# One attention kernel, its side work at steps of its own, maxima and denominators spread over the partitions by DRAM

## The chip, the cores and the metric

The kernel runs on one core of a Trainium2 chip. A core has a matrix engine (TensorE, PE in the profile, with its weight loads as PEld), a vector engine (VectorE, DVE), a scalar engine (ScalarE, ACT), a general engine (GpSimd, POOL) and SyncE (SP), which issues most DMAs. Each engine works through its instructions in the order in which they were written, and waits on semaphores for the others. Matrix products go to PSUM, 8 banks of 2 KB per partition; everything else lies in SBUF or in DRAM. The metric is the time of one execution on the device, in microseconds (us).

## The reference

Four cross-attention layers follow each other on x (2048 tokens of 256 values) with one context (1601 tokens of 512 values). Layers 0, 2 and 3 are alike and called masked here:

```python
q = hidden_states @ Wq            # 16 heads of 64
k = encoder_hidden_states @ Wk
v = encoder_hidden_states @ Wv
logits = jnp.einsum('bhqd,bhkd->bhqk', q, k) * scale
# the columns of a few tokens get -20 * (1 - mask) of the query
probs = jax.nn.softmax(logits + col_bias, axis=-1)
out = jnp.einsum('bhqk,bhkd->bhqd', probs, v)
x = out.reshape(...) @ Wo + bo + x
```

Layer 1, called grouped, normalises x first, has 16 query heads of 16 values over 4 key heads, no mask, and adds its result to x too. All is 32-bit floating point.

## The kernel before, in words

A *block* is two heads of a masked layer (8 blocks a layer) or four of the grouped one (4 blocks, worked two heads at a time). A *unit* is one block, or one pair of heads, for 512 queries: 96 masked and 32 grouped units. A unit has 13 *chunks* of 128 keys (the last has 65).

One loop walks over all chunks of all units; one turn is a *step*. A step does three things for three different units: scores of a chunk of the newest unit (L751), exp of a chunk of the unit before (L834 subtracts the query's maximum on DVE, L841 takes exp on ACT), and the product with the values for a chunk whose exp was done one step earlier (L869). `DELAY` is the number of steps between a unit's last scores and its first exp, here 2; the step of a unit is counted from 0 to 12 by its scores.

In a masked layer scores lie transposed, keys on the partitions: ACT copies them out of PSUM (L763) and DVE keeps the maximum over chunks, still separate for each partition (L768). At step 0 of the next unit PE transposes these (L805), DVE reduces them to one value a query (`ntop`, L806), and at step 1 PE spreads the values over all partitions by transposing broadcast columns (L818) into the PSUM tile `b`, which the subtractions read. POOL adds the probabilities of the chunks (L844 for the first two together, L846 for the others) into `sums`; PE transposes the sums (L888), DVE reduces and inverts them (L889, L890), POOL spreads them along the free axis (`by`, L899), PE transposes that (L907), and DVE multiplies the unit's result with it (L911). Two products with Wo follow (L917), added to x by DVE (L923). In the grouped layer the denominators come out of the product with the values (L894), and maxima are subtracted within the score product.

What is not the pipeline itself is a *piece*: the queries of the next unit (L420), the finish of a unit just named, and the projections of the next block's keys (L369, in slices of 512 columns) and values (L384, chunk by chunk, two to a tile). The class `Pieces` holds queues of them (`urgent`, `fill`, `later`) and hands out about one a step, after the step's three parts. Every product of a piece goes to one PSUM tile, `pm` (pool `ps_m`, one buffer of one bank); the scores, the transposes of the maxima and those of the sums share two tiles of two banks (`ps_s`). The probabilities have 17 buffers (`NP`). The context, transposed, lies in DRAM and comes by DMA in tiles `ct`, three buffers; weights have two buffers.

At the end the order as written is made binding for PE, ACT and DVE. POOL has few instructions and works in the order written too, and so does SP with its DMAs, up to some shifts.

## Time and profile before

| what | value |
| --- | --- |
| median of 3 runs | 5647.72 us (5645.32 to 5651.95) |
| profiled execution | 5653.54 us, its span 5651.8 us |
| PE busy | 5321.4 us, 94% |
| DVE busy | 4013.6 us, 71% |
| ACT busy | 3196.2 us, 57% |
| POOL busy | 2837.7 us, 50% |
| mean granted PE clock | 0.98 of full speed |
| DMA, share of 16 engines | about 15% |

In the profile's lines, L with a number is a line of the kernel. A group line gives the engine, the operation, the tiles written and read (out<-in), how often, the busy time in us and the mean of one in ns, then the idle time before it and what ended it. A line of waits says which engine waited at which line for whom: total us, times, longest. A timeline line gives the start, the time it took, the engine, the line and the tiles, and in brackets the idle time before it with what ended it. A line of DMA issues gives the number of issues, the size of one, and the median time from issue to landing.

### The profile page before, as it was taken

The page shows a single profiled execution, that of the slowest core. Times are in us where ns is not written, and L with a number is a line of the kernel's source. Part 1 is how long each engine was busy: PE and PEld are TensorE (multiplying, and loading weights), DVE is VectorE, ACT ScalarE, POOL GpSimd, SP SyncE. Part 2 cuts the span into 40 slices and gives each one's busy share as a digit, 9 for nine tenths or more (in the row PEclk, how much of TensorE's full clock was granted, in tenths as well). Part 3 has the DMA queues.
Part 4 walks back from the last instruction along what each step waited for, and adds up shares of the span by engine and source line. Part 5 has one row for each costly group of instructions (what it writes and reads, how often), then busy time and mean ns, then how long its engine had stood idle before and what let it go on. Part 6 is the DMA issues. An engine that isn't in the chain of part 4 may idle for free.

```text
span 5651.8 us, 59516 instructions
## 1 busy us (share of the span) xinstructions
PE 5321.4 (94%) x22444; PEld 1865.2 (33%) x22444; DVE 4013.6 (71%) x4140; ACT 3196.2 (57%) x3513; POOL 2837.7 (50%) x1380
## 2 busy tenths in 40 slices
PE   6999999998889999999999999999999999999997
PEld 3333333332323333233233333333333333333332
DVE  3777777777765555555567777777777777777786
ACT  2666666665433434333456666666666666666665
POOL 1766666665410000000056666666666666666676
PEclk8999999999889999999999999999999999999998
DMA  4112211111100000001012111212111121111100
GB/s 135 32 57 60 59 49 53 55 56 44 39 20 5 9 9 9 9 13 52 15 51 61 56 54 49 57 56 59 46 56 55 54 59 49 53 56 52 54 17 15
DMA packets 209744, 252.88 MB, mean 45 GB/s; under 512 B 43529, under 2 KB 155401, under 8 KB 209456
## 3 DMA queue, kind: packets, MB, share of 16 engines
q1 hardware_dynamic: 206192, 243.69, 14.8%
q8 instruction: 177, 2.90, 0.2%
q0 software_dynamic: 1152, 3.28, 0.2%
q10 hardware_dynamic: 2112, 2.10, 0.1%
q14 instruction: 111, 0.91, 0.1%
HBM read 235.27 MB, written 13.76 MB: 44 GB/s over the span
## 4 chain that ended last, share of the span: by engine, by line
PE 78%; ACT 7%; POOL 7%; DVE 5%; issue 2%; DMA 0%; SPq 0%; ACTq 0%; POOLq 0%; DVEq 0%
PE po L869 24%; PE s L751 20%; PE pm L384 6%; PE pm L369 5%; PE pm L917 5%; POOL sums L844 4%; ACT p L763 4%; ACT p L841 3%; POOL sums L846 3%; PE s L850 2%; PE s L784 2%; PE pm L420 2%; PE s L805 2%; PE b L818 2%; PE s L855 2%
## 5 line engine op out<-in xcount | busy, mean ns | idle before, releaser
L846 POOL TENSOR_TENSOR sums<-sums,p 128x1024 f32<-128x1024 f32 (+1 forms) x1056 | 2499.2, 2367 | 1097.9 <-ACT p L841 1084.8
L763 ACT COPY p<-s 128x1024 f32<-128x1024 f32 (+1 forms) x1248 | 1263.4, 1012 | 1434.0 <-PE s L751 1138.3
L869 PE MATMUL po<-p,v 128*64 128x512 f32 (+1 forms) x6656 | 1821.7, 626 | 36.5 <-ACT p L841 34.7
L768 DVE TENSOR_TENSOR top<-s,top 128x1024 f32<-128x1024 f32 (+1 forms) x1056 | 1291.5, 1223 | 753.9 <-ACT p L763 749.4
L751 PE MATMUL s<-q,kT 64*128 64x512 f32 (+1 forms) x4992 | 1426.3, 648 | 117.6 <-DVE top L768 116.4
L834 DVE TENSOR_TENSOR p<-p,b 128x1024 f32<-128x1024 f32 (+1 forms) x1248 | 1504.7, 1206 | 2.4 <-PE b L818 2.0
L841 ACT ACTIVATE p<-p 128x1024 f32<-128x1024 f32 (+1 forms) x1248 | 1321.5, 1059 | 110.3 <-DVE p L834 109.4
L869 PEld LDWEIGHTS po<-p,v 128*64 128x64 f32 (+1 forms) x6656 | 332.0, 136 | 1032.1 <-issue 698.9
L899 POOL COPY by<-rden 128x512 f32<-128x512 f32 x128 | 78.5, 613 | 1111.8 <-DVE rden L897 1083.9
L751 PEld LDWEIGHTS s<-q,kT 64*128 64x128 f32 (+1 forms) x4992 | 370.7, 182 | 732.7 <-issue 454.6
L859 ACT ACTIVATE p<-s 128x1024 f32<-128x1024 f32 (+1 forms) x283 | 289.8, 1024 | 451.0 <-PE s L855 450.9
L844 POOL TENSOR_TENSOR sums<-p 128x1024 f32<-128x1024 f32 x96 | 226.5, 2360 | 434.2 <-ACT p L841 434.2
L789 DVE TENSOR_REDUCE row_top<-s 128x2 f32<-128x1024 f32 x261 | 318.6, 1221 | 122.9 <-PE s L784 121.9
L384 PEld LDWEIGHTS pm<-wv,ct 128*128 128x128 f32 (+1 forms) x2392 | 284.7, 187 | 218.9 <-issue 215.9
L384 PE MATMUL pm<-wv,ct 128*128 128x128 f32 (+1 forms) x2392 | 337.6, 286 | 0.5 <-ACT v L389 0.5
L369 PE MATMUL pm<-ct,wk 128*128 128x512 f32 (+1 forms) x736 | 315.8, 544 | 2.7 <-ACT kT L374 2.7
L917 PE MATMUL pm<-o,wo 128*128 128x512 f32 x512 | 292.0, 653 | 7.1 <-DVE xs L923 2.9
L859 ACT ACTIVATE p<-b 128x1024 f32<-128x1024 f32 (+1 forms) x133 | 136.2, 1024 | 217.8 <-PE b L855 217.8
L923 DVE TENSOR_TENSOR xs<-pm,xs 128x512 f32<-128x512 f32 x232 | 158.4, 683 | 90.4 <-PE pm L917 90.4
L806 DVE TENSOR_REDUCE ntop<-s 128x8 f32<-128x1024 f32 x96 | 117.6, 1225 | 130.9 <-PE s L805 130.6
L789 DVE TENSOR_REDUCE row_top<-b 128x2 f32<-128x1024 f32 x123 | 150.2, 1221 | 62.2 <-PE b L784 61.6
L420 PE MATMUL pm<-xT,wq 128*128 128x512 f32 x336 | 188.5, 644 | 0.0
(191 smaller groups left out, 3279.2 us busy)
## 6 DMA issues: line engine op xcount, KB each, us to landing
ct<-ctxT SPq DMA_DIRECT2D x288, 512.0 KB, 3.8
xT<-xT SPq DMA_DIRECT2D x104, 512.0 KB, 3.5
ct<-ctxT SPq DMA_DIRECT2D x48, 130.0 KB, 2.6
wk<-in_L_xattn_Wk_dram SPq DMA_DIRECT2D x24, 256.0 KB, 4.4
wv<-in_L_xattn_Wv_dram SPq DMA_DIRECT2D x24, 256.0 KB, 3.1
xT<-xs SPq DMA_DIRECT2D x12, 512.0 KB, 2.6
wq<-in_L_xattn_Wq_dram SPq DMA_DIRECT2D x24, 128.0 KB, 2.1
wo<-in_L_xattn_Wo_dram SPq DMA_DIRECT2D x24, 128.0 KB, 2.1
```

The source lines that it names most:

```text
L369: nc.tensor.matmul(u.pk[:, :n], u.wk[:, k, :], ct(k, a, n), start=(k == 0), stop=(k == NCT - 1),)
L384: nc.tensor.matmul(u.pv[:m, c - c0, :], ct(k, a, m), u.wv[:, k, :], start=(k == 0), stop=(k == NCT - 1),)
L751: nc.tensor.matmul(s[:m, h, :], self.u.kT[r, a : a + m], self.q[r, :], start=True, stop=(a != TAIL),)
L763: nc.scalar.copy(p[:m], s[:m])
L768: nc.vector.tensor_tensor(self.top[:m], s[:m], self.top[:m], ALU.max)
L789: nc.vector.tensor_reduce(self.top[:, :, q, k : k + 1], s, AX.X, ALU.max)
L834: nc.vector.tensor_tensor(self.p[c][:m], self.p[c][:m], self.less[:m], ALU.add)
L841: nc.scalar.activation(p[:m], p[:m], AF.Exp)
L844: nc.gpsimd.tensor_tensor(self.sums, self.p[0], p, ALU.add)
L846: nc.gpsimd.tensor_tensor(self.sums[:m], self.sums[:m], p[:m], ALU.add)
L869: nc.tensor.matmul(self.po[r, :], u.v[:m, c, r], self.p[c][:m, h, :], start=(c == 0), stop=(c == NT - 1),)
L917: nc.tensor.matmul(py, wo[:, ts(k, P)], self.o, start=True, stop=True)
```

## The change

- `DELAY` becomes 4 and `NP` 19: exp runs four steps behind the last scores.
- Queries are taken in natural interleaved order: the four transposes of the maxima and of the sums take every fourth query (`columns`), so that partition p holds queries 4p to 4p+3.
- `on_all_partitions` writes such a [128, 2, 4] tile to DRAM (there it is in natural order) and reads it back broadcast over the partitions; SP issues both. The maxima go this way into `spread`, which ACT copies into PSUM at step 3 of the next unit; L818's transposes are gone. The reciprocals of the denominators go this way into `by`; POOL's copy, L907's transposes and DVE's multiply are gone, and POOL multiplies the unit's result in place.
- The transposes of the sums come in two halves, one head each, through `pm` in place of `ps_s`. POOL's sum begins with a copy of chunk 0.
- Keys are projected chunk by chunk (128 columns), values with one tile a chunk, queries in two halves of 256 columns. Each such piece fills and empties its own `pm` tile.
- `Pieces` now has pieces due at steps of their own (`at`), counted for the finish from the step of a unit's last values, which is step 4 of the unit two later: sums at 5 and 6, the multiply at 9, the products with Wo at 11 and 12; queries at 7 and 8; in the grouped layer, stacking at 10 and 11 and a last piece at 12. Chunks of keys and values fill in by a credit in units of cost. A step can hold a due piece and a chunk.
- `wk` and `wv` have one buffer; context tiles are always two chunks wide and loaded three tiles ahead. In the grouped layer the same classes of pieces are cut in the same way.

The core of the diff (blank lines left out):

```diff
-    NP = 17
+    NP = 19
...
-    def context_slice(a, n):
-        step = NCT if n <= 256 else NCT // 2
-        tiles = []
-        for k in range(0, NCT, step):
-            ct = work.tile([P, step, 2 * QB // step], FP, name="ct", bufs=3)
-            nc.sync.dma_start(out=ct[:, :, :n], in_=ctxT_dram[:, k : k + step, a : a + n])
-            tiles.append(ct)
-        return lambda k, b, m: tiles[k // step][:, k % step, b - a : b - a + m]
+    def context_slice(c, held):
+        a = TCH[c][0]
+        n = sum(m for _, m in TCH[c : c + 2])
+        ct = work.tile([P, NCT, 2 * P], FP, name="ct", bufs=3)
+        nc.sync.dma_start(out=ct[:, :, :n], in_=ctxT_dram[:, :, a : a + n])
+        for d in range(len(TCH[c : c + 2])):
+            held[c + d] = lambda k, d=d: ct[:, k, d * P : (d + 1) * P]
...
+            u.wk = weights.tile([P, NCT, P], FP, name="wk", bufs=1)
+            u.wv = weights.tile([P, NCT, P], FP, name="wv", bufs=1)
...
+        def projections(self, u):
+            def keys(c, ct):
                 if u.kT is None:
                     u.kT = heads.tile([P, T], FP, name="kT")
-                if k0 == 0:
-                    u.pk = ps_m.tile([P, 512], FP, name="pm")
-                ct = slices["k", i]
-                for k in range(k0, k1):
+                a, m = TCH[c]
+                pk = ps_m.tile([P, QB], FP, name="pm")[:, :m]
+                for k in range(NCT):
                     nc.tensor.matmul(
-                        u.pk[:, :n], u.wk[:, k, :], ct(k, a, n),
-                        start=(k == 0), stop=(k == NCT - 1),
+                        pk, u.wk[:, k, :], ct(k)[:, :m], start=(k == 0), stop=(k == NCT - 1)
                     )
-                if k1 == NCT:
-                    nc.scalar.copy(u.kT[:, a : a + n], u.pk[:, :n])
-            def values(c, c0, c1):
+                nc.scalar.copy(u.kT[:, a : a + m], pk)
+            def values(c, ct):
                 if u.v is None:
                     u.v = heads.tile([P, NT, P], FP, name="v")
-                if c == c0:
-                    u.pv = ps_m.tile([P, 2, P], FP, name="pm")
-                a, m = TCH[c]
-                ct = slices["v", c0]
+                m = TCH[c][1]
+                pv = ps_m.tile([P, QB], FP, name="pm")[:m, :P]
                 for k in range(NCT):
                     nc.tensor.matmul(
-                        u.pv[:m, c - c0, :], ct(k, a, m), u.wv[:, k, :],
-                        start=(k == 0), stop=(k == NCT - 1),
+                        pv, ct(k)[:, :m], u.wv[:, k, :], start=(k == 0), stop=(k == NCT - 1)
                     )
-                if c == c1 - 1:
-                    nc.scalar.copy(u.v[:m, c0:c1, :], u.pv[:m, : c1 - c0, :])
...
+                nc.scalar.copy(u.v[:m, c, :], pv)
...
+        def query_pieces(self, unit):
             xt = unit.transposed_x()
...
+            half = QB // 2
+            def queries(j):
+                if j == 0:
                     unit.q = heads.tile([P, QB], FP, name="q")
-                    nc.scalar.mul(unit.q, unit.pq, 64 ** -0.5)
-            return [[lambda k=k: queries(k) for k in range(NC)]]
+                part = ts(j, half)
+                pq = ps_m.tile([P, QB], FP, name="pm")[:, :half]
+                for k in range(NC):
+                    nc.tensor.matmul(
+                        pq, unit.u.wq[:, k, :], xt[:, k, part], start=(k == 0), stop=(k == NC - 1)
+                    )
+                nc.scalar.mul(unit.q[:, part], pq, 64 ** -0.5)
+            return [(7 + j, Piece(lambda j=j: queries(j), 1.0)) for j in range(2)]
...
+            return found + [
+                (10, Piece(lambda: stacked(0), 0.5)), (11, Piece(lambda: stacked(1), 0.5)),
+                (12, Piece(last, 0.25)),
+            ]
...
+        return [
+            (9, Piece(squares, 0.0)), (10, Piece(rms, 2.0)),
+            *((11 + q // 2, Piece(lambda q=q: divide(q), 0.0)) for q in range(QT)),
+        ]
...
+    def columns(q):
+        return slice(q, QB, QT)
+    def on_all_partitions(cols, to):
+        rows = dram.tile([2, P, QT], FP, name="cols", bufs=4)
+        with nc.allow_non_contiguous_dma(reason="1024 values, four at a time"):
+            nc.sync.dma_start(out=rows.rearrange("h p q -> p h q"), in_=cols)
+        for tile_, heads_ in to:
+            src = rows[heads_].rearrange("(o h) p q -> o (h p q)", o=1)
+            nc.sync.dma_start(out=tile_, in_=src.to_broadcast(tile_.shape))
...
-                        nc.tensor.transpose(pt[:, h, q, :], self.top[:, h, ts(q, P)], ident)
+                        nc.tensor.transpose(pt[:, h, q, :], self.top[:, h, columns(q)], ident)
                 nc.vector.tensor_reduce(ntop, pt, AX.X, ALU.max, negate=True)
+                self.spread = work.tile([P, 2, QB], FP, name="spread", bufs=1)
+                on_all_partitions(
+                    ntop, [(self.spread.rearrange("n h q -> n (h q)"), slice(0, 2))]
+                )
...
                 self.less = ps_b.tile([P, 2, QB], FP, name="b")
-                for h in range(2):
-                    for q in range(QT):
-                        nc.tensor.transpose(
-                            self.less[:, h, ts(q, P)],
-                            self.ntop[:, h, q : q + 1].to_broadcast((P, P)), ident,
-                        )
+                nc.scalar.copy(self.less, self.spread)
...
-                if c == 1:
+                if c == 0:
                     self.sums = work.tile([P, 2, QB], FP, name="sums")
-                    nc.gpsimd.tensor_tensor(self.sums, self.p[0], p, ALU.add)
-                elif c:
+                    nc.gpsimd.tensor_copy(self.sums, p)
+                else:
                     nc.gpsimd.tensor_tensor(self.sums[:m], self.sums[:m], p[:m], ALU.add)
...
-        def denominators(self):
-            rden = self.rden = small.tile([P, 2, QT], FP, name="rden")
+        def denominators(self, h):
+            if h == 0:
+                self.rden = small.tile([P, 2, QT], FP, name="rden")
+            rden = self.rden
             if self.masked:
-                pt = ps_s.tile([P, 2, QT, P], FP, name="s")
-                for h in range(2):
-                    for q in range(QT):
-                        nc.tensor.transpose(pt[:, h, q, :], self.sums[:, h, ts(q, P)], ident)
-                nc.vector.tensor_reduce(rden, pt, AX.X, ALU.add)
+                pt = ps_m.tile([P, QT, P], FP, name="pm")
+                for q in range(QT):
+                    nc.tensor.transpose(pt[:, q, :], self.sums[:, h, columns(q)], ident)
+                nc.vector.tensor_reduce(rden[:, h, :], pt, AX.X, ALU.add)
+                if h == 0:
+                    return
                 nc.vector.reciprocal(rden, rden)
             else:
                 pd = ps_m.tile([P, QT, 2], FP, name="pm")
                 for q in range(QT):
                     nc.tensor.matmul(
-                        pd[:, q, :], self.oT[:, ts(q, P)], den_rows, start=True, stop=True
+                        pd[:, q, :], self.oT[:, columns(q)], den_rows, start=True, stop=True
                     )
                 nc.vector.reciprocal(rden, pd.rearrange("p q h -> p h q"))
-            self.by = work.tile([P, QT, 2, 64], FP, name="by", bufs=1)
-            nc.gpsimd.tensor_copy(
-                self.by,
-                rden.rearrange("p h (q o) -> p q h o", o=1).to_broadcast((P, QT, 2, 64)),
+            self.by = work.tile([P, QB], FP, name="by", bufs=1)
+            on_all_partitions(
+                rden, [(self.by[self.rows(h)], slice(h, h + 1)) for h in range(2)]
             )
         def divide(self):
-            pr = ps_m.tile([P, QB], FP, name="pm")
-            for q in range(QT):
-                nc.tensor.transpose(
-                    pr[:, ts(q, P)], self.by[:, q].rearrange("p h o -> p (h o)"), ident
-                )
-            self.o = work.tile([P, QB], FP, name="o", bufs=1)
-            nc.vector.tensor_tensor(self.o, pr, self.oT, ALU.mult)
+            nc.gpsimd.tensor_tensor(self.oT, self.oT, self.by, ALU.mult)
...
+        def finish(self):
+            found = [(1 + h, Piece(lambda h=h: self.denominators(h), 0.5)) for h in range(2)]
+            if not self.masked:
+                found = [(1, Piece(lambda: self.denominators(0), 1.0))]
+            found.append((5, Piece(self.divide, 0.0)))
+            return found + [(7 + k, Piece(lambda k=k: self.project(k), 1.0)) for k in range(NC)]
...
+        def at(self, step, found):
+            for steps, piece in found:
+                self.due.setdefault(step + steps, []).append(piece)
+        def step(self, step, share, cost):
+            self.credit = max(min(self.credit + share - cost, 1.5), -1.5)
+            for piece in self.due.pop(step, ()):
+                piece.run()
+                self.credit -= piece.cost
+            while self.fill and self.credit >= self.fill[0].cost / 2:
+                piece = self.fill.popleft()
+                piece.run()
+                self.credit -= piece.cost
...
+        loads, held = deque(), {}
+        def chunks(make, cost):
+            def piece(c):
+                make(c, held[c])
+                if (c % 2 or c == NT - 1) and loads:
+                    loads.popleft()()
+            loads.extend(lambda c=c: context_slice(c, held) for c in range(0, NT, 2))
+            return [Piece(lambda c=c: piece(c), cost(TCH[c][1])) for c in range(NT)]
+        makers = layer.projections(nxt)
+        first, second = [], []
+        if makers:
+            first = chunks(makers[0], lambda m: m / P)
+            second = chunks(makers[1], lambda m: 1.0)
+            for _ in range(3):
+                loads.popleft()()
+        first += layer.own_keys(nxt)
...
-    DELAY, LAG = 2, 1
+    DELAY, LAG = 4, 1
...
+        if top and ca == DELAY - 1:
             top.maxima_spread()
-        if scoring and ca == 2 and ka + 1 < len(units):
+        if scoring and ca == 5 and ka + 1 < len(units):
             ahead = unit_of(ka + 1)
-            pieces.urgent.extend(ahead.layer.unit_groups(ahead))
+            pieces.at(step - ca, ahead.layer.query_pieces(ahead))
         if valuing and cv == NT - 1:
-            pieces.urgent.extend(valuing.finish_groups())
-            pieces.urgent.extend(after(kv))
-        if scoring and ca == 4 and units[ka - 1][:1] == units[ka][:1] != units[ka - 2][:1]:
-            pieces.fill.extend(pieces.later)
-            pieces.later.clear()
-        if scoring and not (top and top.masked):
-            i, b, sub = units[ka]
-            after_this = sum(u[0] == i for u in units[ka + 1 : ka + 8])
-            steps = NT - ca + (NT - 2) * after_this
-            pieces.step(max(1.0, (pieces.left() + 6 * after_this) / steps))
-        elif not scoring:
-            pieces.step(1.0)
-    pieces.flush(pieces.urgent)
+            pieces.at(step, valuing.finish() + after(kv))
+            if units[kv + 1 : kv + 2] and units[kv + 1][0] != units[kv][0]:
+                pieces.release()
+        share = 0.0
+        if scoring:
+            units_left = NB * len(scoring.layer.SUBS) - place - ca / NT
+            own = 6.0 if scoring.masked else 4.6
+            share = (pieces.left() + own * units_left) / (NT * units_left)
+        pieces.step(step, share, 1.0 if top and top.masked and ca == 0 else 0.0)
```

## The prediction

> **What bounds the kernel now.** I read the page's engine line and its chain first, then PE's waits, then the timeline of one unit of a masked layer, then the DMA list.
>
> ```profile
> PE 5321.4 (94%) x22444; PEld 1865.2 (33%) x22444; DVE 4013.6 (71%) x4140; ACT 3196.2 (57%) x3513; POOL 2837.7 (50%) x1380
> ...
> PE 78%; ACT 7%; POOL 7%; DVE 5%; issue 2%; DMA 0%; SPq 0%; ACTq 0%; POOLq 0%; DVEq 0%
> ```
>
> PE is busy 94%, yet it carries only 78% of the chain: other engines hold it up in places. PE's own waits name them.
>
> ```profile
> PE s L751 <- DVE top L768: 116.4, 71, 2.7
> PE pm L907 <- POOL by L899: 55.9, 79, 4.4
> PE po L869 <- ACT p L841: 34.7, 27, 4.1
> ```
>
> Those three make 207 of PE's 330 us of idle time (5651.8 - 5321.4). The list of all engines' waits shows what stands behind the first:
>
> ```profile
> ACT p L763 <- POOL sums L844: 174.5, 93, 2.5
> ```
>
> The buffer of probability chunk 0 is not free until POOL has added chunks 0 and 1. PE's timeline in a masked unit:
>
> ```profile
> 4026.48 1.09 PE L818 MATMUL b<-ident,ntop 128*128 128x128 f32 x8
> 4027.50 1.13 PE L751 MATMUL s<-q,kT 64*128 64x512 f32 x4
> ...
> 4035.82 1.09 PE L888 MATMUL s<-ident,sums 128*128 128x128 f32 x8
> 4038.62 1.13 PE L751 MATMUL s<-q,kT 64*128 64x512 f32 x4 [1.71 <-DVE top L768]
> 4039.68 1.08 PE L869 MATMUL po<-p,v 128*64 128x512 f32 x4
> 4041.38 0.66 PE L907 MATMUL pm<-ident,by 128*128 128x128 f32 x4 [0.62 <-POOL by L899]
> 4041.96 1.13 PE L751 MATMUL s<-q,kT 64*128 64x512 f32 x4
> ```
>
> From start to start, scores cost PE 1.06 us a step, values 1.01, the spread (L818) 1.02, the transposes of the reciprocals (L907) 0.58. The last view is one step on all engines, with a projection (L917) as its piece:
>
> ```profile
> 4002.32 1.13 PE L751 MATMUL s<-q,kT 64*128 64x512 f32 x4
> ...
> 4003.55 1.02 ACT L763 COPY p<-s 128x1024 f32<-128x1024 f32 x1 [1.15 <-PE s L751]
> 4004.39 1.13 PE L917 MATMUL pm<-o,wo 128*128 128x512 f32 x2
> ...
> 4004.60 1.22 DVE L768 TENSOR_TENSOR top<-s,top 128x1024 f32<-128x1024 f32 x1 [0.18 <-ACT p L763]
> ...
> 4005.74 0.68 DVE L923 TENSOR_TENSOR xs<-pm,xs 128x512 f32<-128x512 f32 x1
> ```
>
> Counted from the score's start, PE is done with its piece at 3.12, but DVE empties the piece's PSUM tile only at 4.10, because its maximum of the step stands ahead. There is one such tile ("pm"). A second piece in the same step must wait for it.
>
> **What it removes.** (a) The spread: 96 masked units x 1.01 = 97 us of PE. (b) The reciprocals' transposes: 96 x 0.58 + 32 x 0.49 (grouped layer, 2526.34 to 2526.83) = 71 us. (c) The wait on POOL's `by`: 56 us. (d) The wait behind L844: POOL now copies chunk 0 at once, the probability pool grows with the delay (17 to 19), and the sums' transposes leave the score buffers; of 116 I take 110. What is late next there is the values' wait for exp, below. Together 334 us. On DVE the multiply L911 goes too (88 us), which lies beside PE.
>
> **What it adds on PE.** The instruction order of both versions shows how many pieces fall into each step. Steps with two pieces, one after the other through the one "pm" tile:
>
> (e) 66 steps with half of the sums' transposes and then a chunk of K or V. A half takes 0.51 (half of L888), so the chunk could start at 1.06 + 1.01 + 0.51 = 2.58. DVE's half reduce, about 0.65 (half of 1.216, and the nearest 512-wide row is 0.68), follows the maximum, so the tile is free near 4.1: 1.55 x 66 = 102 us. Lower end 0.5 (POOL or DVE ahead of the row shown), upper 2.5.
>
> (f) 22 steps with a projection, then a V chunk: 4.15 - 3.12 = 1.0 each, 23 us.
>
> (g) Grouped layer, 63 steps with a projection, then a stacking piece: L917 at 2529.12, its DVE add 2530.28 to 2530.97, PE would go on at 2530.09: 0.95 x 63 = 60 us, and some 10 more doubles of its own key pieces, 10 us.
>
> (h) Chunk after chunk, emptied by ACT: 26 pairs, a burst of 13 V chunks before the second block, and the first block's 26 chunks. The rows for such waits are 0.3 us (L369 on kT, 2.7 us in 9) and 0.45 (L384 on v, 1.8 in 4): 0.4 x 65 = 26 us.
>
> (i) K in pieces of 128 columns: a V chunk costs 1.09 from start to start, a quarter of a K slice 1.055; 12 x 24 x 0.035 = 10 us. Queries in halves of 256 have no row; between 0 and 0.1 a unit, I take 5 us.
>
> (j) ACT's new copy into PSUM, 1.02 by L763, stands in its queue behind exp of chunk 12; DVE's first subtract and ACT's first exp wait for it, the copy of `oT` queues behind that, and the next unit's first values wait for both. In 25 units the next step has no piece, and there this comes to about 1 us: 25 us. DVE's two half reduces in neighbouring steps (3.1 and 3.3 us of DVE against 2.58 of PE) cost the 30 units without a double about 0.5: 15 us. Against them stand the 35 us of values' waits shown above, which belong to the old places: together +5 us.
>
> (k) Ends. Two steps more in the drain, where POOL binds at 2.45 a step, against two shorter at the start: 3 us. After the last sums the reciprocals go through DRAM in place of POOL and PE: some 4 us. In the last block, which has no chunks, POOL is near the bound; its copy (1.2, twice the 0.61 of L899) and multiply (1.2, half of 2.37) less `by` 0.61 make 1.8 x 4 = 7 us, and (a) and (b) gain nothing there: 6 us. Together 20 us.
>
> (l) At the change to the grouped layer two of the four normalising parts (0.94 + 2 x 0.64 each) share a step, where each had its own; DVE's sum is the same. I take 8 us, between 0 and 20.
>
> Sum of costs: 102 + 23 + 70 + 26 + 15 + 5 + 20 + 8 = 269. Net 334 - 269 = 65 us off the profiled execution's 5653.5 (span 5651.8 and 1.7 around it), that is 5588. That execution lies 6 us above the median of 5647.7, which is inside the runs' spread of 6.6; I say 5585.
>
> **The round trips at nothing.** Their cover is three steps. The new write (4 KB in pieces of 16 bytes) and the broadcast reads have no row; the nearest are
>
> ```profile
> ct<-ctxT SPq DMA_DIRECT2D x288, 512.0 KB, 3.8
> xT<-xT SPq DMA_DIRECT2D x104, 512.0 KB, 3.5
> ...
> wo<-in_L_xattn_wo_dram SPq DMA_DIRECT2D x16, 16.0 KB, 1.7
> ...
> ctxT<-p SPq DMA_DIRECT2D x2, 65.0 KB, 3.2
> tok_idx<-ttn_token_indices_A_dram SPq DMA_DIRECT2D x3, 1.0 KB, 3.2
> ```
>
> Write 1.7 to 3.2, read 512 KB 3.5 to 7.4 (the slowest 512 KB row of the list, the stores of ctxT). I take 2.4 + 3.6 = 6.0, near the rows of equal size in a quiet stretch (DMA is busy 15 to 20%). The maximum `ntop` is reduced 3.4 us into step 0; ACT's copy could start 3.2 us into step 3, and three steps are 7.2 to 9.4 us: cover 7.0 to 9.2 us. So it is hidden by 1 to 3 us, but at the upper end, 10.6, it is late by 1.4 to 3.6. On SP the write waits for DVE, the read for the write, and behind them the next ct load, which is not due for some steps. Ahead of them at a block's start stand wv and one or two ct loads (some 4 to 8 us of queue, issued one to two steps earlier). For the denominators the cover is longer: reciprocals at 4.4 us of step 6, POOL's multiply after its add at 5.7 of step 9, 14 us later less 4.4. POOL then multiplies until 7.0 of step 9, and PE projects at 7.3 or later; were `by` late, POOL's next adds would queue behind the multiply, and PE's projection behind both.
>
> wk and wv have one buffer each now. SP can load wk only after the last K chunk of the block before, which lies half a block back, and wv after the last V chunk; the first K chunk stands in step 1 to 3, the row for wk is 4.4 us, so this is hidden too. The ct loads stay as many, each of 512 KB.
>
> [...]
>
> **Rivals.**
> 1. *The trip through DRAM is late (slower).* ACT waits for it with the copies of the score buffers behind it, and PE with them. It decides from 65/96 = 0.7 us late in the mean unit on, a trip of about 8.8 us; at 10.6 it is 2.5 x 96 = 240 us, 5825; at 9.5, 1.4 x 96 = 134, about 5720. For it: two dependent transfers, a pattern not in the trace. Against: idle queues.
> 2. *The doubles cost half.* If DVE is ahead, or PE's wait overlaps a wait it has anyway, (e) to (g) are 98 instead of 195: 5490.
> 3. *The change is a wash.* The "pm" tile gives back all that PE saves: 3.0 us per double with a sum, (e) 198: 5681; at 2.5, 5650. For it: evacuations on DVE with a full queue.
> 4. *POOL becomes the bound*: its 12 adds of 2.37, copy and multiply are 31 us of a unit of 42. Only if the multiply beside DVE took 5 us and more; then some 5700. Little for it.
>
> **How the numbers follow.** Forecast (5540 to 5636) 0.46; rival 2 0.15; rival 1 0.22; rival 3 0.13; rival 4 0.04. What a measurement can tell from no change is 0.2%, 11 us. Faster: forecast and rival 2, 0.61, less a little of the forecast's upper end and with some of rival 3's lower: 0.60. Same 0.09, from rival 3 and the weak end of rival 1. Slower 0.31. The range goes from rival 2 (5490, and 10 for its spread) to rival 1 at 9.5 us with 20 for spread: 5480 to 5740. The forecast's own is 5540 to 5636.
>
> **What would show it.** In the new profile: no L818 and L907 groups; PE's wait for `top` near zero; new waits of "pm" matmuls on DVE `rden` and `xs` of about 1.5 and 1 us, some 66 and 85 times; ACT's copy of `spread` without a DMA wait; POOL copies of chunk 0. If ACT waits for the DMA of `spread`, rival 1 holds. If the waits on `rden` are far off 1.5 us, (e) is wrong.

## The result, and the profile after

The forecast was a gain of 1.1%. There is none: the kernel after took 5650.64 us (median of 12 executions, 5638.94 to 5661.18), the kernel before beside it 5649.26 us (12 executions, 5641.72 to 5655.72), a ratio of 1.0005 with an interval of 0.9996 to 1.0013. The profiled execution of after is the fastest of its twelve; its span is 5637.2 us, against 5651.8 before. The working below explains these 14.6 us between two spans; by the medians there is nothing to explain but a zero.

The engine line and the chain of the page after:

```profile
PE 5255.5 (93%) x23412; PEld 2070.8 (37%) x23412; DVE 3981.3 (71%) x4183; ACT 3346.0 (59%) x4096; POOL 3018.6 (54%) x1476
...
PE 80%; DVE 9%; ACT 7%; issue 3%; DMA 1%; POOL 0%; SPq 0%; ACTq 0%; POOLq 0%; DVEq 0%; another core or an unknown queue 0%
```

PE is busy for only 66 us less, although L818 and L907 are gone, and their transposes were 176 us. Its weight loads (PEld) take 206 us more, most because K in chunks of 128 columns and queries in halves load their weights more often (L369 2392 times for 736, 290.3 us for 111.8; L404 672 times for L420's 336, 113.8 us for 50.1), some for another reason that follows below. PE's own waits after, with total us, times and longest:

```profile
PE pm L380 <- DVE rden L893: 50.7, 40, 1.7
PE po L872 <- ACT p L844: 44.3, 39, 5.0
PE po L872 <- ACT oT L878: 33.4, 27, 4.2
PE pm L369 <- DVE rden L893: 32.4, 24, 1.5
PE pm L511 <- DVE xs L922: 22.7, 29, 0.8
PE pm L628 <- DVE xs L922: 22.7, 29, 0.8
PE pm L380 <- DVE xs L922: 20.6, 22, 1.0
```

The scores' wait for `top` and the wait for `by` are gone from the head of the list. In their place stand the doubles (two pieces in one step) that the prediction named: chunks of K and V behind half of the sums (`rden`), stackings (L511, L628) and V chunks behind a projection (`xs`). One such double in the timeline (start, duration, and in brackets the wait before):

```profile
4030.99 0.56 PEld L892 LDWEIGHTS pm<-ident,sums 128*128 128x128 f32 x4 [0.81 <-DVE rden L893]
4031.00 0.75 PE L892 MATMUL pm<-ident,sums 128*128 128x128 f32 x4
4031.33 1.22 DVE L772 TENSOR_TENSOR top<-s,top 128x1024 f32<-128x1024 f32 x1
...
4032.46 0.68 DVE L893 TENSOR_REDUCE rden<-pm 128x4 f32<-128x512 f32 x1
...
4033.20 1.16 PE L380 MATMUL pm<-wv,ct 128*128 128x128 f32 x8 [1.45 <-DVE rden L893]
```

DVE's maximum L772 stands in front of the half reduction L893, so `pm` comes free 1.45 us after PE could have used it, as the prediction argued. What it did not look at is in the groups. First the matrix products and weight loads before:

```profile
L888 PEld LDWEIGHTS s<-ident,sums 128*128 128x128 f32 x768 | 84.4, 141 | 84.9 <-issue 69.5 <-POOL sums L846 15.4
L894 PEld LDWEIGHTS pm<-den_rows,oT 128*128 128x128 f32 x256 | 31.0, 191 | 26.0 <-issue 25.2 <-ACT p L763 0.8
```

and the same work after, where the columns are every fourth query:

```profile
L892 PEld LDWEIGHTS pm<-ident,sums 128*128 128x128 f32 x768 | 108.2, 209 | 164.9 <-POOL sums L847 70.6 <-issue 47.7 <-DVE rden L893 36.9
L900 PEld LDWEIGHTS pm<-den_rows,oT 128*128 128x128 f32 x256 | 62.1, 327 | 26.8 <-issue 26.8
```

Each transpose has one weight load (768, eight in each of 96 units). With every fourth query, in steps of 16 bytes, one takes 209 ns instead of 141, and in the grouped denominators 327 instead of 191.

The table counts PE's time from the start of each product to the start of the next, less idle time, in the two profiled executions. With some 11 us ahead of the first and behind the last product it adds up to the spans.

| part of PE's time | before, us | after, us | difference |
| --- | --- | --- | --- |
| spread L818, transposes L907 | 176.4 | 0 | -176.4 |
| transposes of sums L888 / L892 | 103.0 | 137.3 | +34.3 |
| transposes of maxima L805 / L809 | 99.8 | 110.9 | +11.1 |
| grouped denominators L894 / L900 | 29.4 | 60.6 | +31.2 |
| K chunks L369 | 315.8 | 343.0 | +27.2 |
| V chunks L384 / L380 | 330.2 | 339.8 | +9.6 |
| projections L917 / L916 | 268.5 | 280.3 | +11.8 |
| scores and values | 3046.0 | 3026.8 | -19.2 |
| all other products | 951.9 | 956.4 | +4.5 |
| idle between products | 320.0 | 371.0 | +51.0 |

Scores and values are the same instructions in both kernels; the mean granted clock was 0.980 before and 0.984 after.

### The profile page after: what moved, and what is told of

Its sections match the earlier page's. It is cut to its first block, busy times and chain, and to the rows that moved or that the text cites. A ratio compares the mean times of both kernels' runs of the same rounds, so it can differ in the third digit from the quotient of the medians.

```text
span 5637.2 us, 63697 instructions
## 1 busy us (share of the span) xinstructions
PE 5255.5 (93%) x23412; PEld 2070.8 (37%) x23412; DVE 3981.3 (71%) x4183; ACT 3346.0 (59%) x4096; POOL 3018.6 (54%) x1476
## 3 DMA queue, kind: packets, MB, share of 16 engines
q1 hardware_dynamic: 338288, 328.53, 20.6%
q14 instruction: 127, 1.04, 0.1%
## 4 chain that ended last, share of the span: by engine, by line
PE 80%; DVE 9%; ACT 7%; issue 3%; DMA 1%; POOL 0%; SPq 0%; ACTq 0%; POOLq 0%; DVEq 0%; another core or an unknown queue 0%
PE po L872 24%; PE s L755 20%; PE pm L369 6%; PE pm L380 6%; PE pm L916 4%; PE pm L404 4%; ACT p L767 3%; DVE p L837 2%; PE s L853 2%; PE s L788 2%; PE s L809 2%; ACT p L844 2%; PE s L858 2%; DVE top L772 2%; PE pm L892 1%
## 5 line engine op out<-in xcount | busy, mean ns | idle before, releaser
L849 POOL TENSOR_TENSOR sums<-sums,p 128x1024 f32<-128x1024 f32 (+1 forms) x1152 | 2725.1, 2366 | 1089.6 <-ACT p L844 1012.1
L872 PE MATMUL po<-p,v 128*64 128x512 f32 (+1 forms) x6656 | 1813.3, 624 | 83.8 <-ACT p L844 44.3
L772 DVE TENSOR_TENSOR top<-s,top 128x1024 f32<-128x1024 f32 (+1 forms) x1056 | 1291.6, 1223 | 680.4 <-ACT p L767 678.6
L844 ACT ACTIVATE p<-p 128x1024 f32<-128x1024 f32 (+1 forms) x1248 | 1322.0, 1059 | 169.5 <-DVE p L837 163.3
L910 POOL TENSOR_TENSOR oT<-oT,by 128x512 f32<-128x512 f32 x128 | 163.8, 1280 | 1160.8 <-DMA by<-cols 901.1
L380 PE MATMUL pm<-wv,ct 128*128 128x128 f32 (+1 forms) x2392 | 344.4, 287 | 78.9 <-DVE rden L893 50.7
L380 PEld LDWEIGHTS pm<-wv,ct 128*128 128x128 f32 (+1 forms) x2392 | 286.6, 187 | 284.7 <-issue 142.0
L369 PE MATMUL pm<-ct,wk 128*128 128x128 f32 (+1 forms) x2392 | 346.0, 288 | 45.8 <-DVE rden L893 32.4
L369 PEld LDWEIGHTS pm<-ct,wk 128*128 128x128 f32 x2392 | 290.3, 191 | 258.3 <-issue 175.6
L916 PE MATMUL pm<-oT,wo 128*128 128x512 f32 x512 | 292.2, 653 | 13.3 <-POOL oT L910 12.5
L383 ACT COPY v<-pm 128x128 f32<-128x128 f32 (+1 forms) x312 | 82.2, 264 | 186.8 <-PE pm L380 179.0
L847 POOL COPY sums<-p 128x1024 f32<-128x1024 f32 x96 | 99.5, 1037 | 170.6 <-ACT p L844 170.6
```

The lines of the kernel that those rows point to most:

```text
L369: nc.tensor.matmul(pk, u.wk[:, k, :], ct(k)[:, :m], start=(k == 0), stop=(k == NCT - 1))
L380: nc.tensor.matmul(pv, ct(k)[:, :m], u.wv[:, k, :], start=(k == 0), stop=(k == NCT - 1))
L772: nc.vector.tensor_tensor(self.top[:m], s[:m], self.top[:m], ALU.max)
L844: nc.scalar.activation(p[:m], p[:m], AF.Exp)
L849: nc.gpsimd.tensor_tensor(self.sums[:m], self.sums[:m], p[:m], ALU.add)
L872: nc.tensor.matmul(self.po[r, :], u.v[:m, c, r], self.p[c][:m, h, :], start=(c == 0), stop=(c == NT - 1),)
```

## The experiments

Unless something else is said, each run was timed five times beside nine executions of the kernel before. Differences are taken between the ratios to before, one percent being 56.5 us.

**Consecutive queries in the denominators.** In the kernel after:

```diff
-                    nc.tensor.transpose(pt[:, q, :], self.sums[:, h, columns(q)], ident)
+                    nc.tensor.transpose(pt[:, q, :], self.sums[:, h, ts(q, P)], ident)
...
-                        pd[:, q, :], self.oT[:, columns(q)], den_rows, start=True, stop=True
+                        pd[:, q, :], self.oT[:, ts(q, P)], den_rows, start=True, stop=True
```

> Only the transposes of the sums (L892) and the denominators' products (L900) read consecutive queries again in place of every fourth, so that the denominators belong to the wrong queries; the maxima stay strided. Theory 1 (the stride makes PE's weight loads longer: in the changed kernel L892 takes 137 us of PE from start to start against 103 for L888 before, L900 61 against 29): 34 + 31 = 65 us less, about 5585, weight loads of L892 back from 209 to about 140 ns. Rival (PE waits for DVE in these steps anyway, so the masked part is hidden): 31 us less, about 5620. Rival (the stride is not the cause, the loads are long for another reason): no change, 5650.

Measured: 5613.11 us, ratio 0.9925 [0.9912, 0.9939], some 45 us below the kernel after. The same two groups of weight loads in this run:

```profile
L892 PEld LDWEIGHTS pm<-ident,sums 128*128 128x128 f32 x768 | 83.4, 145 | 167.5 <-POOL sums L847 69.0 <-issue 51.7 <-DVE rden L893 36.1
L900 PEld LDWEIGHTS pm<-den_rows,oT 128*128 128x128 f32 x256 | 31.8, 195 | 26.8 <-issue 26.8
```

The loads fall back to 145 and 195 ns: it is the stride. PE's time in L900 falls from 60.6 to 33.3, in L892 from 137.3 to 121.6 only. The other 19 us of L892 above the 103.0 of before stay. They probably go with the halves, in which four transposes instead of eight follow each other; no run has the halves alone, but the kernel before agrees: its transposes in fours (L907) took 0.154 us of PE each, its transposes in eights (L888) 0.134, and these, in fours, 0.158. And 8 us of the gain went back into the waits for `rden` (83 to 91 us): a chunk that is sooner at the tile waits longer for it.

**The same stride put into the kernel before.**

```diff
-                        nc.tensor.transpose(pt[:, h, q, :], self.sums[:, h, ts(q, P)], ident)
+                        nc.tensor.transpose(pt[:, h, q, :], self.sums[:, h, q::QT], ident)
...
-                        pd[:, q, :], self.oT[:, ts(q, P)], den_rows, start=True, stop=True
+                        pd[:, q, :], self.oT[:, q::QT], den_rows, start=True, stop=True
```

> The kernel before with one thing changed: the transposes of the sums (L888) and the grouped denominators' products (L894) load every fourth query instead of 128 in a row, as the change does. Nothing else moves. (What comes out belongs to other queries, so the denominators are put to wrong ones; the instructions are otherwise the same.) Theory (a strided load of a TensorE weight costs TensorE's time, whatever stands around it): L888 from 103 to about 119 us and L894 from 29 to about 60, 45 us in all above the kernel before. Rival (the difference seen between the two kernels came with the half tiles and the places of the pieces): within 10 us of the kernel before.

Measured: 5672.05 us beside 5644.91, ratio 1.0048 [1.0034, 1.0062], 27 us slower. In this run:

```profile
L888 PEld LDWEIGHTS s<-ident,sums 128*128 128x128 f32 x768 | 101.5, 208 | 83.9 <-issue 68.4 <-POOL sums L846 15.5
L894 PEld LDWEIGHTS pm<-den_rows,oT 128*128 128x128 f32 x256 | 62.2, 327 | 26.0 <-issue 25.1 <-ACT p L763 0.8
```

208 and 327 ns, with everything else as before: the stride alone makes the price, and the rival (half tiles and places) falls. PE's time is +12 us in L888 and +31 in L894. That is 43, of which 27 arrived; the scores' wait for `top`, which stands in other places of the same steps, was 10 us shorter, and scores and values ran 8 us faster. A load in steps of 16 bytes thus cost 67 and 136 ns more than one of consecutive values. No run tries another stride, and why this one costs it is not shown here.

**Consecutive queries everywhere, with the order made in DRAM.** In the kernel after all transposes read 128 consecutive queries, and the write to DRAM puts them in order:

```diff
-        return slice(q, QB, QT)
+        return ts(q, P)
...
-            nc.sync.dma_start(out=rows.rearrange("h p q -> p h q"), in_=cols)
+            nc.sync.dma_start(out=rows.rearrange("h q p -> p h q"), in_=cols)
```

> All three kinds of strided loads gone, and the order kept right by writing to DRAM in pieces of 4 bytes (1024 of them) in place of 16 bytes (256). Theory 1: 77 us less than the changed kernel, about 5573, if the longer write stays hidden; the write takes 2.4 us in the changed kernel, its cover is 1 to 3 us more. Rival (the write grows by more than 3 us): ACT's copy of spread waits for its DMA and the gain is eaten; from 0.8 us late in the mean unit on nothing is left.

Measured: 6922.08 us, ratio 1.2247 [1.2230, 1.2264]. The DMA issues (times, size, median us from issue to landing) and ACT's waits:

```profile
spread<-cols SPq DMA_DIRECT2D x96, 512.0 KB, 4.6
by<-cols SPq DMA_DIRECT2D x256, 128.0 KB, 3.9
...
cols<-rden SPq DMA_DIRECT2D x128, 4.0 KB, 10.1
cols<-ntop SPq DMA_DIRECT2D x96, 4.0 KB, 9.7
```

```profile
ACT p L767 <- POOL sums L849: 694.0, 195, 9.0
ACT b L824 <- DMA spread<-cols: 538.4, 93, 10.7
```

The same 4 KB in pieces of 4 bytes take 9.7 to 10.1 us to land; in the kernel after, in pieces of 16, 2.4. This is the prediction's first rival, made to happen: a trip of 9.7 + 4.6 = 14.3 us against a cover of 7.0 to 9.2, and with it a trip of 14.0 for the denominators, cost more than a fifth of the time before. Leaving out the waits over 20 us in and around the grouped layer, which both kernels have, POOL's multiply waited 765 us for `by` in 96 waits, against 50 in 16 in the kernel after, and ACT's copies of the scores waited for POOL's additions behind it. The clock was lower too, 0.899. The interleaved order is therefore no whim. It buys the write of 2.4 us and pays for it with the strided loads.

**No chunk in a step that has a due piece.** In `Pieces.step` of the kernel after:

```diff
-            for piece in self.due.pop(step, ()):
+            due = self.due.pop(step, ())
+            for piece in due:
...
-            while self.fill and self.credit >= self.fill[0].cost / 2:
+            busy = any(piece.cost for piece in due)
+            while not busy and self.fill and self.credit >= self.fill[0].cost / 2:
```

> The changed kernel, but a chunk of keys or values is not filled into a step that has a due piece with a cost: the 66 steps with a sum's transposes and a chunk are gone, 25 more pairs of chunks appear. Theory 1 (one PSUM tile, emptied by DVE behind its maximum): the 85 us of PE's waits on rden go, about 10 come back between chunks: 75 us less, about 5575. Rival (DVE is the bound in those two steps, 3.1 and 3.3 us against 2.7 of PE, and PE waits for exp instead): 35 us less, about 5615.

Measured: 5557.22 us, ratio 0.9833 [0.9819, 0.9846], 97 us below the kernel after. The waits for `rden` are gone from PE's list, whose next entries did not grow:

```profile
PE po L872 <- ACT p L844: 43.2, 40, 5.0
PE po L872 <- ACT oT L878: 23.2, 11, 4.2
PE pm L511 <- DVE xs L922: 22.7, 29, 0.8
PE pm L628 <- DVE xs L922: 22.7, 29, 0.8
PE pm L380 <- DVE xs L922: 20.5, 22, 0.9
```

So the chunks have room elsewhere, and the 66 doubles were a pure loss. The gain is 12 us more than their 85: the values' wait for `oT` fell by 10, for 17 chunks now stand in steps that had no piece (see (j) below). The 22 V chunks behind a projection stay (20.5 us): `flush` hands them out at the change of a block, which this edit leaves alone.

**Stackings moved away from the projections as well.** On top of the last edit:

```diff
-                (10, Piece(lambda: stacked(0), 0.5)), (11, Piece(lambda: stacked(1), 0.5)),
-                (12, Piece(last, 0.25)),
+                (9, Piece(lambda: stacked(0), 0.5)), (10, Piece(lambda: stacked(1), 0.5)),
+                (14, Piece(last, 0.25)),
```

> The kernel after, with no chunk of fill in a step that has a due piece with cost, and with the grouped queries' two stackings one step earlier and their last piece at step 14, so that they no longer stand directly behind a projection in `pm`. In the run with the first of these edits alone (5557 us) the stackings and the last piece still waited 52 us for the projections' additions (`pm` L511 and L628 <- DVE `xs` L920 and L922). Theory (these waits are a cost of where the pieces stand): they go, 5557 - 50 = about 5507 us. Rival (another piece stands behind the additions instead): within 15 us of 5557.

Measured: 5481.74 us beside 5648.31, ratio 0.9707 [0.9694, 0.9720], 71 us below the last run where 50 were expected. The waits of L511 and L628 for `xs` went, and PE's time in the projections came back to 269.5 us from 280: a stacking right behind a projection had cost there too. With these pieces apart the change is a gain of 2.9%.

**POOL's copy alone, in the kernel before.**

```diff
-                if c == 1:
+                if c == 0:
...
-                    nc.gpsimd.tensor_tensor(self.sums, self.p[0], p, ALU.add)
-                elif c:
+                    nc.gpsimd.tensor_copy(self.sums, p)
+                else:
```

> The kernel before with one edit: POOL copies chunk 0 into the sums in place of adding chunks 0 and 1 together. This is term (d) alone. Theory 1 (the stall at the sums is the buffer of chunk 0 held by POOL): PE's 116 us of waits for top go, 110 us less, about 5539. Rival (the sums' transposes take one of the two score tiles, so a shorter wait for top stays, about 0.45 us in 96 units): 70 us less, about 5580. Rival (POOL, with 1 us more a unit, is late for the sums): less than 40.

Measured: 5538.74 us beside 5654.44, ratio 0.9801 [0.9788, 0.9815], 2.0% faster by two lines. Most of step (d) needs neither the delay nor DRAM. ACT's waits for POOL's L844 are gone, and PE's wait for `top` is 29.4 us (71 times) instead of 116.4:

```profile
PE pm L907 <- POOL by L899: 62.9, 96, 3.1
PE po L869 <- ACT p L841: 33.5, 25, 4.1
PE s L751 <- DVE top L768: 29.4, 71, 1.6
```

That the time came out as expected is luck in part. The waits for `top` fell by 87 us, not by 110: the rival's shorter wait stayed, 0.41 us in 71 units. The rest came from PE itself. Its instructions are the same as before, yet its time between starts fell from 5321 to 5278 us. Some 15 of these 43 us stand at L784 and L850, where this trace lacks 102 records and cannot be compared; the other 28 us are real, 25 of them in scores and values, with a mean granted clock of 0.986 against 0.980.

**The maxima by way of DRAM, in the kernel before.** On top of the copy, with `DELAY` 4 and 19 buffers of `p`:

```diff
-                        nc.tensor.transpose(pt[:, h, q, :], self.top[:, h, ts(q, P)], ident)
+                        nc.tensor.transpose(pt[:, h, q, :], self.top[:, h, slice(q, QB, QT)], ident)
...
+                on_all_partitions(
+                    ntop, [(self.spread.rearrange("n h q -> n (h q)"), slice(0, 2))]
+                )
...
-                for h in range(2):
-                    for q in range(QT):
-                        nc.tensor.transpose(
-                            self.less[:, h, ts(q, P)],
-                            self.ntop[:, h, q : q + 1].to_broadcast((P, P)), ident,
-                        )
+                nc.scalar.copy(self.less, self.spread)
```

> The kernel before with only two parts of the change: POOL copies chunk 0 as it comes, and the maxima go by way of DRAM (strided transposes L805, one write, one read, ACT into `b`), with the exps four steps behind and two more `p` tiles. Denominators, `by`, projections and all chunks stay as before. To fit, the context weights have one buffer instead of two and the quotient is put into `oT`. Against the copy alone (5539 us): the spread transposes L818 go (97.6 us), the strided transposes cost 11, the ends 20. Theory (the maxima's part of the change is a gain by itself, and its cost is in the other parts): about 70 us below the copy alone, 5470 us. Rival (the values' longer waits for ACT, 47 us in the kernel after, come with ACT's copies and the longer chain): 20 us below the copy alone, 5520 us.

Measured: 5483.83 us, ratio 0.9708 [0.9695, 0.9722], 53 us below the copy alone, nearer to the theory (70) than to the rival (20). PE's waits:

```profile
PE pm L917 <- POOL by L909: 59.7, 93, 3.1
PE po L879 <- ACT p L851: 39.2, 38, 4.7
PE s L762 <- DVE top L779: 36.2, 86, 2.0
```

The values (L879) wait 43 us in all, near the 36.5 of before: ACT's copies into PSUM and the longer delay do not make the 83.8 us of the kernel after by themselves. This run has the old denominators and the old queues of pieces and is as fast as the one with the new ones and its pieces apart (0.9708 and 0.9707). So the second round trip, with the halves and the new places that came with it, gained nothing over the old way; the two kernels differ in more than the trip, which alone was not measured. On PE it saves little: L888, L894 and L907 together were 211 us of its time before, L892 and L900 are 198 after.

**One piece between denominators and division.** On top of the last run:

```diff
-            return [[self.denominators], [self.divide]] + [
+            return [[self.denominators], [pieces.another], [self.divide]] + [
```

where `another` takes one piece of fill. In this version what waited for `by` was the transposes, so they are moved and nothing is taken away.

> As the run with the copy and the maxima by way of DRAM in the kernel before (5484 us), with one piece of fill run between a unit's denominators and its division, so that POOL's `by` is ready when TensorE comes to transpose it (L917 waited 59.7 us, 93 times, for POOL). Theory (the wait goes, no other takes its place): 5430 us. Rival (a piece of fill put there waits for a tile instead, or the later projections are waited for): within 15 us of 5484.

Measured: 5441.10 us beside 5644.91, ratio 0.9643 [0.9630, 0.9656], the fastest of all and 37 us below the last run, between the theory's 54 and the rival's 15. The wait at the transposes fell from 59.9 to 6.2 us; 18 of it came back at the projections, which now wait for the division.

```profile
PE po L879 <- ACT p L851: 42.6, 45, 5.9
PE s L762 <- DVE top L779: 35.2, 84, 1.7
PE s L898 <- POOL sums L856: 17.4, 8, 9.0
PE pm L926 <- DVE oT L920: 16.1, 11, 3.5
```

**Two that were slower.** The first takes the strides, the halves and the second trip out at once, on top of the run with the pieces apart:

```diff
-                pt = ps_m.tile([P, QT, P], FP, name="pm")
-                for q in range(QT):
-                    nc.tensor.transpose(pt[:, q, :], self.sums[:, h, columns(q)], ident)
-                nc.vector.tensor_reduce(rden[:, h, :], pt, AX.X, ALU.add)
+                for h in range(2):
+                    nc.tensor.matmul(
+                        pd[self.rows(h), :], ones[:, :64], self.sums[:, h, :],
+                        start=True, stop=True,
+                    )
...
+            nc.vector.reciprocal(self.by, pd)
```

> As the run with the pieces apart, but the sums' transposes (L892), the grouped denominators' products with strided columns (L900), the reduction and the second round trip through DRAM are taken out. In their place two products of a 128x64 block of ones with `sums` (one for each head, into one `pm`) and, for grouped blocks, one product of a selector with `oT`; DVE takes the reciprocal of the whole 128x512 tile into `by`, and POOL multiplies as in the kernel after. TensorE: L892 133 and L900 64 us go; 192 products of 512 columns at the values' 0.26 us and 32 at a projection's 0.55 us come, 67 us. Theory (what the strided reads cost is TensorE's time): 130 us below the run with the pieces apart. Rival: the reciprocal, at least the 0.68 us of an addition of that shape and perhaps several times that, holds up the subtractions and `pm`, and a half or more of the 130 us is lost.

Measured: 5670.86 us, ratio 1.0046 [1.0032, 1.0060], 191 us above the run with the pieces apart. The rival held:

```profile
L902 DVE RECIPROCAL by<-pm 128x512 f32<-128x512 f32 x128 | 428.9, 3351 | 76.4 <-PE pm L898 52.3 <-PE pm L893 24.0
```

A reciprocal of 128x512 takes 3.35 us on DVE, five times the 0.68 us of an addition of that shape, and `pm` is held as long: the chunks of K and V wait 147 us for it. PE's gain was smaller than expected too: the masked products took 0.51 us each and not 0.26 (98 us for 192), so that 130 us of products replace 197.

The second was to test whether ACT's copies cause the values' waits, by letting DVE subtract from SBUF:

```diff
-                self.less = ps_b.tile([P, 2, QB], FP, name="b")
-                nc.scalar.copy(self.less, self.spread)
+                self.less = self.spread
```

> The kernel after, but DVE subtracts the maxima straight from `spread` in SBUF (two buffers), and ACT's copy into `b` (96 of 1.0 us) is gone. To fit, the context tiles have two buffers instead of three. Theory (the values' longer waits, 83.8 us against 36.5 in the kernel before, come from ACT's copies, for which the subtractions wait 71 us): 30 to 47 us below the kernel after. Rival (DVE with both operands in SBUF, beside POOL's additions, takes longer than the 1.21 us of a subtraction from PSUM): no gain, or slower.

Measured: 6162.68 us, ratio 1.0910 [1.0896, 1.0925]. DVE's subtraction and POOL's additions:

```profile
L836 DVE TENSOR_TENSOR p<-p,spread 128x1024 f32<-128x1024 f32 (+1 forms) x1248 | 2707.1, 2170 | 0.6
...
L848 POOL TENSOR_TENSOR sums<-sums,p 128x1024 f32<-128x1024 f32 (+1 forms) x1152 | 3417.0, 2966 | 838.6 <-ACT p L843 751.9 <-DMA by<-cols 8.6 <-ACT q L407 8.2
```

With both operands in SBUF a subtraction takes 2.17 us instead of the 1.21 of the kernel after, and POOL's addition 2.97 instead of 2.37. The longer time comes with POOL beside it: the 25 subtractions of this trace during which POOL ran nothing took 1.21 to 1.23 us. The run says nothing on the values' waits, but it shows what ACT's copy into PSUM is for.

## Why the prediction was wrong

The step that failed is the price of the new work on TensorE. Step (i) was all of it, 15 us (K chunks 10, halves of the queries 5), and 130 came; only the halves of the queries cost what they were priced at, 3.5 us. The transposes were carried over as the same instructions with another index, at no cost. By the table, L892, L809 and L900 are 77 us above their old forms; the two runs with the stride changed put 43 us on the stride of L892 and L900 (16 and 27 taken out, 12 and 31 put in), and the run of consecutive queries leaves 19 that probably go with the halves. K chunks cost 27 and not 10, for a quarter of the old slice took 1.012 us (315.8 in 312 parts) and not the 1.055 that was read off the timeline, and a chunk takes 1.10; V chunks were 10 us dearer, why is not shown; projections 12, of which the run with the pieces apart took back 11.

The other steps against the two traces:

- (a), (b), (c): 97.6, 78.8 and 56.1 us, expected 97, 71 and 56. Right.
- (d): the scores' idle time fell from 117.6 to 5.7 us, 112 where 110 was expected. Right: by the copy alone 87 of the 116 went. The 29 that stayed went in the kernel after, whose sums' transposes leave the score buffers; the run with the maxima by way of DRAM, which keeps them there, still had 36. That PE also runs faster, by 28 us in the run of the copy, was in no term.
- (e): 66 waits, 85 us in all, 1.3 each. Expected 66 at 1.55, 102 us. Right in its mechanism, a fifth too large.
- (f): 20.6 us in 22, expected 23. (g): 52 us at the stackings in 64, expected 60 in 63. Right.
- (h): 26 us (11.9, 6.6, 4.6 and 3.2), expected 26. Right.
- (j): the cost was right, what was set against it was not. The values' waits rose by 47 us, expected 5. The path that the prediction named is in the trace: in the 25 units whose next step has no piece, the first values wait for `oT`, whose copy stands behind ACT's copy into PSUM, a subtraction and exp. That is 28 us in the 25 places: 0.7 once a block in 17 of them, 1.6 to 1.7 in six units at both ends, 4.1 and 2.2 in two more. Expected were 25 us in 25. In the 66 units with a chunk in that step these waits are 0.1 us in all, and the run with the maxima by way of DRAM, which has a piece there in its masked units, shows none of 0.7. One of the 17, with the scores directly before the values:

```profile
3981.91 1.08 PE L872 MATMUL po<-p,v 65*64 65x512 f32 x4
3982.92 1.13 PE L755 MATMUL s<-q,kT 64*128 64x512 f32 x4
3984.74 1.08 PE L872 MATMUL po<-p,v 128*64 128x512 f32 x4 [0.69 <-ACT oT L878]
```

  What failed is the 35 us of old waits that were to go. Three quarters of them stand where the masked layer meets the grouped one (1290 to 1630 us), and there the waits over 0.4 us sum to 26 before and 40 after. Why these stayed and grew is open.
- The round trips at nothing: right. ACT's copies waited 3.8 us for `spread` in all, the write took 2.4 us as taken, the reads 3.7 and 3.1. The first trip was thus 6.1 us, against the 6.0 taken. Rivals 1 and 4 did not occur.
- (k) and (l), 28 us together, were not measured apart.

In sum: the removed products and waits came to 353 us (176 and 177; predicted 334). The new waits were 228 us (predicted 254, all of (e) to (l) but (i)). The new time on TensorE was 130 us (predicted 15), less 19 by which scores and values ran faster, beside a clock of 0.984 for 0.980. -353 + 228 + 130 - 19 = -14, the difference of the two spans. Rival 3, the wash, named the right outcome by the wrong way: the doubles did not cost 2.5 to 3.0 us each. What is true of it is that they were needless. They and the stackings behind projections cost 168 us by the runs (1.0005 to 0.9707), more than the 137 us of waits that PE's list showed for them; 10 of `oT` and 11 of the projections' time went with them.

## What to carry to other kernels

A changed index is a changed instruction: a transpose's weight load took 209 ns with every fourth query and 141 with consecutive ones. Look for the row of a load with that stride, and where there is none, price it from both sides and not at nothing. With one PSUM tile for all side work, a list of pieces to a step is a price list: two in one step cost the time until the first is emptied (1.3 us each in the 66 steps of (e)), and moving one of them cost nothing here, where other steps were empty. Take a bundle of edits apart before judging it; here two lines gave 2.0%, and two of the parts with one moved piece 3.6%, while the whole gave nothing.

## What the runs showed of the hardware

- A 128x128 weight load of 4-byte values in steps of 16 bytes took 209 ns against 141 for consecutive ones, and 327 against 191 where only two columns are multiplied with it.
- A 4 KB write to DRAM took 2.4 us in pieces of 16 bytes and, in the run with the order made in DRAM, 9.7 to 10.1 in pieces of 4.
- DVE's reciprocal of 128x512 from PSUM took 3.35 us; its addition of that shape 0.68.
- DVE's subtraction of 128x1024 with both operands in SBUF took 2.17 us on average, mostly beside POOL, and 1.22 where POOL ran nothing, as much as from PSUM (1.21). POOL's addition took 2.97 for 2.37.
- POOL copied 128x1024 in 1.04 us, where an addition of that shape takes 2.37. The prediction had taken 1.2.
- The mean granted clock rose from 0.980 to 0.986 in the run of the copy alone, where PE's stalls at the scores fell from 118 to 31 us. The slowest kernels (6922 and 6163 us) had 0.899 and 0.959. PE's idle time alone does not order the clocks: the kernel after has 51 us more of it than the kernel before and 0.984. Why was not tested.
